# A gated cross-attention block on one core: the last two row pairs of the feed-forward part put into a written order

## The chip, the core and the metric

The kernel runs on one core of a Trainium2 chip. A core has five engines with a queue each: TensorE (PE in the profile; PEld is its weight load), VectorE (DVE), ScalarE (ACT), GpSimd (POOL), and SyncE (SP), which here only starts transfers. They run side by side and meet at semaphores. Inside one queue instructions run in the order of the program, so an instruction that waits holds up all that stand behind it on its engine. The metric is the device time of the whole kernel in microseconds; lower is better.

## What is computed

Sixteen sequences of 224 rows (512 wide) attend to a context of up to 750 rows (384 wide), of which a mask keeps only some; then each row passes a two-layer feed-forward net with quantised operands. Cut to what matters:

```python
def attention(x, context, mask, W_q, W_k, W_v, W_o, b_o):   # 8 heads of 64
    q, k, v = x @ W_q, context @ W_k, context @ W_v
    sim = where(mask, einsum(q, k) * 64**-0.5, -max)
    return einsum(softmax(sim), v) @ W_o + b_o

def bitlinear(x, w, b):
    xq = act_quant(rmsnorm(x))      # to 8-bit steps by the row's largest magnitude
    return xq @ weight_quant(w).T + b                       # weights to -1, 0, 1

def ffn(x): return bitlinear(gelu(bitlinear(x, w1, b1)), w2, b2)    # 512 -> 2048 -> 512

x = x + tanh(g_xattn) * attention(layernorm(x), context, ...)
x = x + tanh(g_ffn) * ffn(layernorm(x))
```

## The kernel before

**Work units.** The 16 sequences are ordered by how many context rows the mask keeps, and one sequence is a *slot* s (0 to 15). The 3584 rows in slot order are cut into 28 tiles of 128 rows; two tiles make a *pair* i (0 to 13), and k (0 or 1) is the tile within it. A slot's attention needs its queries, keys and values, the scores of four units (`scores`, L1088 and L1098), the turn of the probabilities by TensorE (`turn_probs`, L1128) and the weighted sum (`weighted`, L1151), whose result goes to the ring buffer `xoT`.

**What a pair passes through.** `residual` gathers the rows of x by an indirect transfer that GpSimd issues (L807) and adds the bias (L1207). `project(i, k)` multiplies `xoT` by W_o in float32 (L1214) and adds to the rows y (L1217). `normalise` takes mean and largest magnitude (L1251 to L1255), makes the quantising scale (`quantiser`, L1225 and L1226), rounds to integers (L1260) and turns them into bfloat16 (L1261); a transfer on SP's queue transposes them (L1262); GpSimd computes the scale that is multiplied back (`unquantiser`, L1233 to L1235). `up(i, k, g)` is the first layer for half g of 2048 columns (L1284), with a DVE add that takes the result out of PSUM (L1292). `gelu(i, ks)` runs Gelu on ACT (L1315), takes the largest magnitude (L1318), quantises (L1321), casts (L1324), transposes by a transfer on SP (L1325), and measures the mean square on ACT (L1344). `down` is the second layer (L1424, sixteen matmuls), and `store` adds into y (L1436) and sends the tile with an indirect transfer that GpSimd issues (L1438). The indirect stores wait for one another: each one waits until the store before it has landed.

**Two forms of a transpose.** The transposes of `xq` and `hq` go through a transfer on SP for most pairs. For the last two pairs, 12 and 13, `hq` is transposed by TensorE instead (`turn_by_tensor`: L1304, sixteen small matmuls, and two ACT copies at L1305).

**The order.** The main loop over slots hands three streams of pieces (attention of this slot; preparation of the next; feed-forward pieces of earlier pairs) to `merge`, which interleaves them by a planned cost each. In slot 15 the feed-forward stream is the residual of pair 12, `up` and `gelu` of pair 11, `project` and `normalise` of pair 12, and `down` of pair 11. After the loop comes the end, with what is left: the residual, projection and normalisation of pair 13; `up` of pair 12; `up_last` of pair 13 (as `up`, with Gelu and the largest magnitude by halves: L1366, L1374, L1377, L1378); `down` of pair 12 and of pair 13 with TensorE transposes woven in; four stores. The layer that builds the program still orders each engine's instructions by itself; `tc.issue_after(x)` keeps what is written in its block behind x on x's engine. It is order only and adds no semaphore.

Names of instructions below: `hp_12_0_1` is the up product of pair 12, tile 0, half 1; `fp` a down product; `op` a projection; `hq`, `hqT` the quantised middle rows and their transpose; `xq`, `xqT` the same for the input of the first layer; `c_2` the scale that `store` multiplies back.

Of the kernel before, what the change touches and what calls it, by code (L numbers as in the profile page):

```python
# [733 lines left out]
def compact_path(ctx, tc, sh, x, context, out, late_loads, stages):  # L734
# [405 lines left out]
    def weighted(s):  # L1140

        st = live[s]
        rest = CAPS[s] > P
        av = wide([P, 2, NB], F32, f"av_{s}")
        by = av[:, :, : 2 * S].rearrange("p a (i q) -> p a i q", i=2)
        for a in range(2):
            for i in range(2):
                p = 2 * a + i
                for j in range(2):
                    rows = slice((a ^ j) * DH, ((a ^ j) + 1) * DH)  # L1150
                    nc.tensor.matmul(  # L1151
                        by[rows, a, i, :],
                        lhsT=st["v"][:, (2 * p + j) * DH : (2 * p + j + 1) * DH],
                        rhs=st["pT"][:, 2 * p + j, :],
                        start=(i == 0),
                        stop=(not rest and i == 1),
                    )
        if rest:

            for i in range(2):  # L1160
                for a in range(2):
                    p = 2 * a + i
                    for j in range(2):
                        keys = slice(j * DH, (j + 1) * DH)
                        rows = slice((a ^ j) * DH, ((a ^ j) + 1) * DH)
                        nc.tensor.matmul(
                            by[rows, a, i, :],
                            lhsT=st["v_rest"][keys, p, :],
                            rhs=st["pT"][keys, 8 + p, :],
                            start=False,  # L1170
                            stop=(i == 1),
                        )
        at = (s % 4) * S
        for a in range(2):
            evict(xoT[:, 2 * a : 2 * a + 2, at : at + S], by[:, a], 2 * S)
# [33 lines left out]
    def project(i, k):  # L1209
        y = pairs[i]["y"]  # L1210
        at = (2 * i + k) * P % RING
        po = gen([P, D], F32, f"op_{i}_{k}")
        for d in range(ND):
            nc.tensor.matmul(  # L1214
                po, lhsT=xoT[:, d, at : at + P], rhs=sh.wo[:, d, :], start=(d == 0), stop=(d == ND - 1)
            )
        nc.vector.scalar_tensor_tensor(y[:, k, :], po, sh.tgates[:, 0:1], y[:, k, :], ALU.mult, ALU.add)  # L1217
        load["v"] += 700


# [9 lines left out]
    def unquantiser(amax, r, part, isw, name):  # L1230

        c = small(f"c_{name}")
        nc.gpsimd.tensor_tensor(c[:, part], amax[:, part], r[:, part], ALU.mult)  # L1233
        nc.gpsimd.tensor_scalar(c[:, part], c[:, part], 1e-5, None, ALU.max)
        nc.gpsimd.tensor_scalar(c[:, part], c[:, part], isw, None, ALU.mult)  # L1235
        return c

    def normalise(i, ks=(0, 1)):
# [20 lines left out]
        for k in ks:  # L1259
            nc.vector.tensor_scalar(xq.bitcast(I16)[:, k, :], fx[:, k, :], scale[:, k : k + 1], None, ALU.mult)  # L1260
        nc.vector.tensor_copy(xq[:, part, :], xq.bitcast(I16)[:, part, :])  # L1261
        nc.sync.dma_start_transpose(  # L1262
            out=xqT[:, ks[0] * ND : (ks[-1] + 1) * ND, :], in_=xq[:, part, :].rearrange("p n d -> p (n d)")
        )

# [7 lines left out]
        load["v"] += len(ks) * (850 + 340 + 667 + 450 + 220)  # L1273

    def up(i, k, g):
# [5 lines left out]
        for n in range(2):  # L1281
            at = (2 * g + n) * NB
            for d in range(ND):
                nc.tensor.matmul(  # L1284
                    ph[:, n, :],
                    lhsT=f["xqT"][:, k * ND + d, :],
                    rhs=w1T[:, d, at : at + NB],
                    start=(d == 0),
                    stop=(d == ND - 1),
                )  # L1290
# [3 lines left out]
        )  # L1294
        load["v"] += 1280

    def turn_by_tensor(i, k):
# [10 lines left out]
    def gelu(i, ks=(0, 1)):  # L1308
# [5 lines left out]
        for k in ks:  # L1314
            nc.scalar.activation(f["h", k], f["h", k], AF.Gelu)  # L1315
        for k in ks:
# [6 lines left out]
            if i < NPAIR - 2:  # L1323
                nc.vector.tensor_copy(hq, hq.bitcast(I16))  # L1324
                nc.sync.dma_start_transpose(out=hqT, in_=hq)  # L1325
                continue
            half = FF // 2
            for g in range(2):
                cols = slice(g * half, (g + 1) * half)
                nc.scalar.copy(hq[:, cols], hq.bitcast(I16)[:, cols])  # L1330
            f["hq", k] = hq
        f["ss", ks], f["a2", ks] = ss, amax
        if i < NPAIR - 2:
            measure(i, ks)
        load["v"] += len(ks) * (2282 + 1280 + 690)
        load["s"] += len(ks) * 2 * 1910 + 2600

    def measure(i, ks):
        f = pairs[i]
        name = f"{i}_{ks[0]}"  # L1340
        part = slice(ks[0], ks[-1] + 1)
        ss, amax = f["ss", ks], f["a2", ks]
        for k in ks:
# [5 lines left out]
        for k in ks:  # L1349
            f["c2", k] = c[:, k : k + 1]  # L1350

    def up_last(i, k):
# [8 lines left out]
        for g in range(2):  # L1361
            ph = wide([P, 2, NB], F32, f"hp_{i}_{k}_{g}")
            for n in range(2):
                at = (2 * g + n) * NB
                for d in range(ND):
                    nc.tensor.matmul(  # L1366
                        ph[:, n, :],
                        lhsT=f["xqT"][:, k * ND + d, :],
                        rhs=w1T[:, d, at : at + NB],
                        start=(d == 0),  # L1370
                        stop=(d == ND - 1),
                    )
# [5 lines left out]
            nc.vector.tensor_reduce(most[:, g : g + 1], h[:, cols], AX.X, ALU.max, apply_absolute_value=True)  # L1378
        f["h", k], f["most", k] = h, most

    def gelu_last(i, k):
# [11 lines left out]
        for g in range(2):  # L1393
            cols = slice(g * half, (g + 1) * half)
            nc.vector.tensor_scalar(hq.bitcast(I16)[:, cols], h[:, cols], scale[:, part], None, ALU.mult)
            rounded = nc.vector.tensor_copy(hq[:, cols], hq.bitcast(I16)[:, cols])
        f["hq", k], f["a2", k] = hq, amax
        return rounded.ins

    def measure_last(i, k):  # L1400
        f = pairs[i]
        name = f"{i}_{k}"
        part = slice(k, k + 1)
        squares = small(f"sq_{name}")
        for g in range(2):
# [6 lines left out]
            )  # L1412
        r = small(f"r2_{name}")
        nc.gpsimd.tensor_tensor(r[:, part], squares[:, 0:1], squares[:, 1:2], ALU.add)
        nc.gpsimd.tensor_scalar(r[:, part], r[:, part], 1.0 / FF, EPS, ALU.mult, ALU.add)
        pow_half(r[:, part])
        c = unquantiser(f["a2", k], r, part, sh.isw[1], f"2_{name}")
        f["c2", k] = c[:, part]

    def down(i, k, between=None):  # L1420
        f = pairs[i]
        po = gen([P, D], F32, f"fp_{i}_{k}")
        for n in range(NF):
# [3 lines left out]
            if between and n == NF // 2 - 1:  # L1427
                with tc.issue_after(last.ins):
                    f["turned"] = turn_by_tensor(*between)
        f["po", k] = po  # L1430

    def store(i, k):
        f = pairs[i]
        po = f["po", k]
        y = f["y"][:, k, :]
        nc.vector.scalar_tensor_tensor(y, po, f["c2", k], y, ALU.mult, ALU.add)  # L1436
        load["v"] += 700
        nc.gpsimd.indirect_dma_start(  # L1438
            out=out_rows,
# [4 lines left out]
            oob_is_err=False,  # L1444
        )
    NPAIR = NTOK // 2

# [14 lines left out]
    def project_pieces(i):  # L1462
        p = [(1.8, lambda k=k: project(i, k)) for k in range(2)]
        return p + [(0.0, lambda: normalise(i))]


# [177 lines left out]
    for s in range(B):  # L1644
# [10 lines left out]
        else:  # L1655
# [4 lines left out]
            if complete:  # L1660
                flow.append((0.0, lambda i=projected: residual(i)))
            if raised < projected:
                flow += up_pieces(raised)
                raised += 1
            if complete:
                flow += project_pieces(projected)
# [14 lines left out]
    residual(i)  # L1681
    for k in range(2):
        project(i, k)
        normalise(i, (k,))
    ups = up_pieces(i - 1)
    for k in range(2):
        for _, piece in ups[3 * k : 3 * k + 3]:
            piece()
    for k in range(2):
        up_last(i, k)  # L1690
    measure(i - 1, (0,))
    turn_by_tensor(i - 1, 0)
# [12 lines left out]
    store(i, 0)  # L1705
    with tc.issue_after(pairs[i]["turned"]):
        measure_last(i, 1)
    down(i, 1)
# [35 lines left out]
```

## Time and profile before

| | us |
|---|---|
| three timed runs: median (lowest to highest) | 751.87 (750.98 to 754.66) |
| the profiled execution, whole | 748.97 |
| its span, first to last instruction | 747.2 |
| start of the last store's issue, and its end | 734.90, 736.0 |
| from there to the end of the span (no compute instruction) | 11.2 |

| busy, us (share of the span) | PE | PEld | DVE | ACT | POOL |
|---|---|---|---|---|---|
| whole span | 682.8 (91%) | 436.8 (58%) | 497.6 (67%) | 420.0 (56%) | 396.4 (53%) |

Where a timeline row is shown, it gives the start in us from the start of the span, the duration in us, engine, line, operation, what it writes and reads (names without numbers), shapes, the count, and in brackets how long the engine had been idle before it and what ended the idle time. Times near the end of the span are what this change is about: it touches slot 15 (from about 648 us) and all that comes after it.

### The profile page before, as it was taken

What the parts mean: (1) busy time and instruction counts of PE and PEld (TensorE: products, weight loads), DVE (VectorE), ACT (ScalarE), POOL (GpSimd) and SP (SyncE); (2) the same over time, 40 slices, a digit from 0 to 9 for tenths busy, and PEclk for the clock granted to TensorE, in tenths of its full rate; (3) what the DMA queues carried; (4) which work ended last, traced back from release to release, by engine and by line L of the source; (5) the groups of instructions that cost most, each with busy time, mean ns of one, the idle gap of its engine ahead of it and who ended that gap; (6) DMA issues with size and microseconds to landing.
All of it is one profiled execution on the core that took longest, in us unless ns stands there. A gap on an engine that the chain in (4) does not pass through costs nothing.

```text
span 747.2 us, 11515 instructions
## 1 busy us (share of the span) xinstructions
PE 682.8 (91%) x3964; PEld 436.8 (58%) x3964; DVE 497.6 (67%) x1290; ACT 420.0 (56%) x981; POOL 396.4 (53%) x543
## 2 busy tenths in 40 slices
PE   4998899999999999997999999999999999988780
PEld 3786677675656565655555675666666566443330
DVE  5586846866684684755768675588594939586950
ACT  2549645383673846636757368366565656461680
POOL 5583676463654644547366564565654453536142
PEclk9989999999999999999999999999999999999996
DMA  7794031222222312222142323124122222213000
GB/s 244 272 292 130 29 87 32 15 73 57 81 45 60 95 43 73 52 59 80 28 100 68 78 61 68 42 68 85 55 57 71 57 71 54 75 29 78 7 26 35
DMA packets 78898, 56.67 MB, mean 76 GB/s; under 512 B 67168, under 2 KB 67312, under 8 KB 78704
## 3 DMA queue, kind: packets, MB, share of 16 engines
q1 hardware_dynamic: 70704, 29.90, 17.5%
q0 software_dynamic: 8128, 25.96, 10.9%
q8 instruction: 33, 0.54, 0.3%
q14 instruction: 33, 0.27, 0.1%
HBM read 32.26 MB, written 7.34 MB: 53 GB/s over the span
## 4 chain that ended last, share of the span: by engine, by line
PE 52%; DVE 13%; issue 12%; POOL 10%; ACT 6%; DMA 4%; POOLq 0%; ACTq 0%; DVEq 0%
PE qp L1035 9%; PE op L1214 8%; PE fp L1424 7%; PE hp L1284 6%; PE kp L916 4%; PE sim L1074 4%; PE vp L931 4%; PE ptp L1128 2%; PE av L1151 2%; POOL p L1108 2%; DVE a L1318 2%; DMA out_dram<-y,token 2%; DVE h L1292 2%; DVE hq L1321 1%; DVE p L1088 1%
## 5 line engine op out<-in xcount | busy, mean ns | idle before, releaser
L1108 POOL TENSOR_TENSOR p<-p,rec 112x768 f32<-112x768 f32 (+1 forms) x64 | 84.3, 1318 | 71.7 <-DVE rec L1107 29.1
L1098 ACT ACTIVATE p<-p,nm 112x192 f32<-112x192 f32 (+1 forms) x256 | 106.5, 419 | 8.0 <-DVE nm L1088 7.8
L1424 PE MATMUL fp<-w2T,hqT 128*128 128x512 fp8e4 x448 | 103.4, 384 | 7.9 <-ACT hqT L1305 4.0
L1035 PE MATMUL qp<-xnT,wq_sb 128*128 128x224 f32 x512 | 105.0, 359 | 0.6 <-ACT xnT L780 0.6
L1214 PE MATMUL op<-wo_sb,xoT 128*128 128x512 f32 x224 | 103.7, 599 | 0.0
L1284 PE MATMUL hp<-w1T,xqT 128*128 128x512 fp8e4 x416 | 99.8, 384 | 3.4 <-DVE nm L1088 1.9
L1035 PEld LDWEIGHTS qp<-xnT,wq_sb 128*128 128x128 f32 x512 | 96.9, 193 | 6.4 <-issue 3.3
L1292 DVE SCALAR_TENSOR_TENSOR h<-hp,c,b_bc 128x1024 f32<-128x1024 f32 x52 | 66.5, 1280 | 38.3 <-PE hp L1284 38.0
L1088 DVE CUSTOM_DVE_ANT_0 p<-sim,mask 112x128 f32<-112x128 f32 (+1 forms) x224 | 57.9, 313 | 34.0 <-PE sim L1074 33.7
L1424 PEld LDWEIGHTS <-hqT 128*128 128x128 bf16 x448 | 42.8, 99 | 62.4 <-issue 7.5
L1318 DVE TENSOR_REDUCE a<-h 128x1 f32<-128x2048 f32 x26 | 59.3, 2282 | 22.4 <-ACT h L1315 22.3
L1436 DVE SCALAR_TENSOR_TENSOR y<-fp,c,y 128x512 f32<-128x512 f32 x28 | 20.9, 746 | 78.0 <-PE fp L1424 66.5
L1284 PEld LDWEIGHTS <-xqT 128*128 128x128 bf16 x416 | 40.3, 98 | 48.6 <-issue 10.2
L1438 POOL DMA_INDIRECT out_dram<-y,token x28 | 30.7, 1095 | 62.6 <-DVE y L1436 51.6
L1214 PEld LDWEIGHTS op<-wo_sb,xoT 128*128 128x128 f32 x224 | 40.6, 190 | 38.9 <-issue 36.4
L916 PE MATMUL kp<-ctxT,wk_sb 128*128 128x192 f32 (+1 forms) x384 | 63.1, 313 | 0.0
L916 PEld LDWEIGHTS kp<-ctxT,wk_sb 128*128 128x128 f32 x384 | 57.5, 198 | 6.2 <-issue 4.3
L1344 ACT ACTIVATE h<-h 128x2048 f32<-128x2048 f32 x26 | 49.7, 1910 | 17.1 <-DVE hq L1321 9.6
L1272 POOL TENSOR_TENSOR y<-y,b_bc 128x512 f32<-128x512 f32 x28 | 36.6, 1312 | 38.3 <-DVE fx L1253 38.0
L780 ACT COPY pT<-ptp 128x448 f32<-128x448 f32 x62 | 32.3, 536 | 42.4 <-PE ptp L1128 42.3
L1315 ACT ACTIVATE h<-h 128x2048 f32<-128x2048 f32 x26 | 49.6, 1909 | 9.0 <-DVE h L1292 8.8
L1074 PE MATMUL sim<-kT,qT 64*112 64x192 f32 (+1 forms) x512 | 50.9, 313 | 1.0 <-DVE nm L1088 0.6
(195 smaller groups left out, 1223.3 us busy)
## 6 DMA issues: line engine op xcount, KB each, us to landing
raw<-in_L_ffn_w_dram SPq DMA_DIRECT2D x16, 512.0 KB, 5.3
wq_sb<-in_L_xattn_W_q_dram SPq DMA_DIRECT2D x1, 1024.0 KB, 5.7
b_bc<-in_L_ffn_b_dram SPq DMA_DIRECT2D x1, 1024.0 KB, 8.0
wk_sb<-in_L_xattn_W_k_dram SPq DMA_DIRECT2D x1, 768.0 KB, 7.3
wv_sb<-in_L_xattn_W_v_dram SPq DMA_DIRECT2D x1, 768.0 KB, 8.7
wo_sb<-in_L_xattn_W_o_dram SPq DMA_DIRECT2D x1, 512.0 KB, 3.7
wo_sb<-in_L_xattn_W_o_dram SPq DMA_DIRECT2D x2, 256.0 KB, 5.7
y<-in_x_dram,token POOLq DMA_INDIRECT x28, 3.5
```

Source lines behind the costliest of these rows:

```text
L916: nc.tensor.matmul(pk[:, p - p0, :], lhsT=sh.wk[:, c, p * P : (p + 1) * P], rhs=st["ctxT"][:, c, :cap], start=(c == 0), stop=(c == NC - 1),)
L1035: nc.tensor.matmul(pq[:, i, :], lhsT=sh.wq[:, d, (p + i) * P : (p + i + 1) * P], rhs=st["xnT"][:, d, :], start=(d == 0), stop=(d == ND - 1),)
L1074: nc.tensor.matmul(sim[:, j, i, :cap], lhsT=st["qT"][j * DH : (j + 1) * DH, p, q * TQ : (q + 1) * TQ], rhs=st["kT"][j * DH : (j + 1) * DH, ...
L1088: nc.vector.tensor_tensor_reduce(out=probs[:, h, :cap], in0=sim[:, j, i, :cap], in1=st["mask"][:, j * begin : j * begin + cap], scale=-(DH ...
L1098: nc.scalar.activation(probs[:, h, :cap], probs[:, h, :cap], AF.Exp, bias=nmax, scale=-1.0, accum_out=total[:TQ, h : h + 1],)
L1108: nc.gpsimd.tensor_tensor(probs[:, :, :cap], probs[:, :, :cap], rec[:TQ].unsqueeze(2).to_broadcast([TQ, 4, cap]), ALU.mult,)
L1214: nc.tensor.matmul(po, lhsT=xoT[:, d, at : at + P], rhs=sh.wo[:, d, :], start=(d == 0), stop=(d == ND - 1))
L1284: nc.tensor.matmul(ph[:, n, :], lhsT=f["xqT"][:, k * ND + d, :], rhs=w1T[:, d, at : at + NB], start=(d == 0), stop=(d == ND - 1),)
L1292: nc.vector.scalar_tensor_tensor(h[:, cols], ph.rearrange("t i n -> t (i n)"), f["c1", k], sh.b1[:, cols], ALU.mult, ALU.add)
L1318: nc.vector.tensor_reduce(amax[:, k : k + 1], h, AX.X, ALU.max, apply_absolute_value=True)
L1344: nc.scalar.activation(f["h", k], f["h", k], AF.Square, accum_out=ss[:, k : k + 1])
L1424: last = nc.tensor.matmul(po, lhsT=f["hqT", k][:, n, :], rhs=w2T[:, n, :], start=(n == 0), stop=(n == NF - 1))
```

## The change

The last slot's feed-forward stream and the end are written out as one sequence. Pair 12 goes up in front of the projection of pair 13; its down product is split around the way up of pair 13; pair 11's second down product moves out of slot 15 into the end; the input rows of pair 13 are transposed by TensorE (`turn_rows`) instead of by a transfer, and tile 0 of pair 12's middle rows by a transfer instead of by TensorE. The mean square of h_12_1 and of pair 13 is computed apart from the scale that is multiplied back (`mean_square`, `measure_last`). `project`, `up`, `up_last`, `down`, `normalise` and `store` return instructions, so that later ones can be put behind them. Lines that only do that are left out here, and so is `gelu_last`, where a return value goes.

```diff
@@ normalise
-        nc.sync.dma_start_transpose(
-            out=xqT[:, ks[0] * ND : (ks[-1] + 1) * ND, :], in_=xq[:, part, :].rearrange("p n d -> p (n d)")
-        )
+        if i < NPAIR - 1:
+            nc.sync.dma_start_transpose(
+                out=xqT[:, ks[0] * ND : (ks[-1] + 1) * ND, :], in_=xq[:, part, :].rearrange("p n d -> p (n d)")
+            )
...
+    def turn_rows(i, k):
+
+        f = pairs[i]
+        pt = gen([P, ND, P], BF16, f"xqp_{i}_{k}")
+        for d in range(ND):
+            nc.tensor.transpose(pt[:, d, :], f["xq"][:, k, d * P : (d + 1) * P], ident16)
+        nc.scalar.copy(f["xqT"][:, k * ND : (k + 1) * ND, :], pt)
@@ gelu
         for k in ks:
-            nc.scalar.activation(f["h", k], f["h", k], AF.Gelu)
+            if (i, k) != (NPAIR - 2, 1):
+                nc.scalar.activation(f["h", k], f["h", k], AF.Gelu)
...
             if i < NPAIR - 2:
-                nc.vector.tensor_copy(hq, hq.bitcast(I16))
+                late["rounded"] = nc.vector.tensor_copy(hq, hq.bitcast(I16)).ins
+            else:
+                for g in range(2):
+                    cols = slice(g * FF // 2, (g + 1) * FF // 2)
+                    nc.scalar.copy(hq[:, cols], hq.bitcast(I16)[:, cols])
+            f["hq", k] = hq
+            if (i, k) != (NPAIR - 2, 1):
                 nc.sync.dma_start_transpose(out=hqT, in_=hq)
...
+        if (i, ks[0]) == (NPAIR - 2, 1):
+            f["a2", 1] = amax[:, 1:2]
+            return
@@ down
             if between and n == NF // 2 - 1:
                 with tc.issue_after(last.ins):
-                    f["turned"] = turn_by_tensor(*between)
+                    between()
@@ new
+    def last_slot(i):
+
+        ups = up_pieces(i - 1)
+
+        def norm(k):
+            late["normed"] = normalise(i, (k,))
+
+        def gelu_behind():
+            with tc.issue_after(late["normed"]):
+                gelu(i - 1, (1,))
+
+        p = ups[:5]
+        for k in range(2):
+            p += [(1.8, lambda k=k: project(i, k)), (0.0, lambda k=k: norm(k))]
+        return p + [(0.0, gelu_behind)] + down_pieces(i - 1)[:1]
@@ the slot loop
-            if raised < projected:
+            if s == B - 1:
+                flow += last_slot(projected)
+            elif raised < projected:
@@ the end
     i = NPAIR - 1
     residual(i)
-    for k in range(2):
-        project(i, k)
-        normalise(i, (k,))
-    ups = up_pieces(i - 1)
-    for k in range(2):
-        for _, piece in ups[3 * k : 3 * k + 3]:
-            piece()
-    for k in range(2):
-        up_last(i, k)
-    measure(i - 1, (0,))
-    turn_by_tensor(i - 1, 0)
-    down(i - 1, 0, (i - 1, 1))
-    down(i - 1, 1)
-    with tc.issue_after(pairs[i - 1]["turned"]):
-        measure(i - 1, (1,))
-    rounded = [gelu_last(i, k) for k in range(2)]
-    for k in range(2):
-        with tc.issue_after(rounded[k]):
-            store(i - 1, k)
-    with tc.issue_after(pairs[i - 1]["turned"]):
+    with tc.issue_after(late["av"]), tc.issue_after(late["rounded"]):
+        for k in range(2):
+            for g in range(2):
+                raised = up(i - 1, k, g)
+            if k == 0:
+                gelu(i - 1, (0,))
+    f = pairs[i - 1]
+    nc.scalar.activation(f["h", 1], f["h", 1], AF.Gelu)
+    mean_square(i - 1, 1)
+    with tc.issue_after(raised):
+        lowered = down(i - 2, 1)
+    store(i - 2, 1)
+    with tc.issue_after(lowered):
+        for k in range(2):
+            projected = project(i, k)
+            normed = normalise(i, (k,))
+    with tc.issue_after(normed):
+        gelu(i - 1, (1,))
+    measure_last(i - 1, 1)
+    with tc.issue_after(projected):
+        lowered = down(i - 1, 0, lambda: turn_rows(i, 0))
+    with tc.issue_after(lowered):
+        up_last(i, 0)
+        mean_square(i, 0)
+        turn_rows(i, 1)
+        raised = up_last(i, 1)
+    store(i - 1, 0)
+    with tc.issue_after(raised):
+        turn_by_tensor(i - 1, 1)
+        lowered = down(i - 1, 1)
+    mean_square(i, 1)
+    added, sent = store(i - 1, 1)
+    gelu_last(i, 0)
+    with tc.issue_after(added):
+        gelu_last(i, 1)
+    with tc.issue_after(raised):
+        turn_by_tensor(i, 0)
+    with tc.issue_after(sent):
         measure_last(i, 0)
-    turn_by_tensor(i, 0)
-    down(i, 0, (i, 1))
-    store(i, 0)
-    with tc.issue_after(pairs[i]["turned"]):
-        measure_last(i, 1)
+        measured = measure_last(i, 1)
+    with tc.issue_after(lowered):
+        down(i, 0, lambda: turn_by_tensor(i, 1))
+    with tc.issue_after(measured):
+        store(i, 0)
     down(i, 1)
     store(i, 1)
```

`mean_square` holds the two ACT squares of half a tile and the three GpSimd steps up to the inverse root, which stood at the head of `measure_last` before.

More of the change, by code (lines that the diff above doesn't have):

```diff
@@ L1150, in weighted @@
                     rows = slice((a ^ j) * DH, ((a ^ j) + 1) * DH)
-                    nc.tensor.matmul(
+                    last = nc.tensor.matmul(
                         by[rows, a, i, :],
@@ L1165, in weighted @@
                         rows = slice((a ^ j) * DH, ((a ^ j) + 1) * DH)
-                        nc.tensor.matmul(
+                        last = nc.tensor.matmul(
                             by[rows, a, i, :],
@@ L1172, in weighted @@
                         )
+        late["av"] = last.ins
         at = (s % 4) * S
@@ L1213, in project @@
         for d in range(ND):
-            nc.tensor.matmul(
+            last = nc.tensor.matmul(
                 po, lhsT=xoT[:, d, at : at + P], rhs=sh.wo[:, d, :], start=(d == 0), stop=(d == ND - 1)
@@ L1218, in project @@
         load["v"] += 700
+        return last.ins
     def quantiser(amax, part, least, name):
@@ L1234, in unquantiser @@
         nc.gpsimd.tensor_scalar(c[:, part], c[:, part], 1e-5, None, ALU.max)
-        nc.gpsimd.tensor_scalar(c[:, part], c[:, part], isw, None, ALU.mult)
+        latest["p"] = nc.gpsimd.tensor_scalar(c[:, part], c[:, part], isw, None, ALU.mult).ins
         return c
@@ L1260, in normalise @@
             nc.vector.tensor_scalar(xq.bitcast(I16)[:, k, :], fx[:, k, :], scale[:, k : k + 1], None, ALU.mult)
-        nc.vector.tensor_copy(xq[:, part, :], xq.bitcast(I16)[:, part, :])
-        nc.sync.dma_start_transpose(
-            out=xqT[:, ks[0] * ND : (ks[-1] + 1) * ND, :], in_=xq[:, part, :].rearrange("p n d -> p (n d)")
-        )
+        rounded = nc.vector.tensor_copy(xq[:, part, :], xq.bitcast(I16)[:, part, :])
+        if i < NPAIR - 1:
+            nc.sync.dma_start_transpose(
+                out=xqT[:, ks[0] * ND : (ks[-1] + 1) * ND, :], in_=xq[:, part, :].rearrange("p n d -> p (n d)")
+            )
         r = small(f"r1_{name}")
@@ L1273, in normalise @@
         load["v"] += len(ks) * (850 + 340 + 667 + 450 + 220)
+        return rounded.ins
+    def turn_rows(i, k):
[4 more added lines that the diff above has]
+        nc.scalar.copy(f["xqT"][:, k * ND : (k + 1) * ND, :], pt)
     def up(i, k, g):
@@ L1283, in up @@
             for d in range(ND):
-                nc.tensor.matmul(
+                last = nc.tensor.matmul(
                     ph[:, n, :],
@@ L1295, in up @@
         load["v"] += 1280
+        return last.ins
     def turn_by_tensor(i, k):
@@ L1323, in gelu @@
             if i < NPAIR - 2:
-                nc.vector.tensor_copy(hq, hq.bitcast(I16))
-                nc.sync.dma_start_transpose(out=hqT, in_=hq)
[L1326 to L1342, printed above, removed]
+                late["rounded"] = nc.vector.tensor_copy(hq, hq.bitcast(I16)).ins
[5 more added lines that the diff above has]
+            if (i, k) != (NPAIR - 2, 1):
+                nc.sync.dma_start_transpose(out=hqT, in_=hq)
+        if (i, ks[0]) == (NPAIR - 2, 1):
+            f["a2", 1] = amax[:, 1:2]
+            return
         for k in ks:
@@ L1350, in measure @@
             f["c2", k] = c[:, k : k + 1]
+        load["v"] += len(ks) * (2282 + 1280 + 690)
+        load["s"] += len(ks) * 2 * 1910 + 2600
     def up_last(i, k):
@@ L1365, in up_last @@
                 for d in range(ND):
-                    nc.tensor.matmul(
+                    last = nc.tensor.matmul(
                         ph[:, n, :],
@@ L1379, in up_last @@
         f["h", k], f["most", k] = h, most
+        return last.ins
     def gelu_last(i, k):
@@ L1395, in gelu_last, with mean_square @@
             nc.vector.tensor_scalar(hq.bitcast(I16)[:, cols], h[:, cols], scale[:, part], None, ALU.mult)
[L1396 to L1400, printed above, removed]
+            nc.vector.tensor_copy(hq[:, cols], hq.bitcast(I16)[:, cols])
+        f["hq", k], f["a2", k] = hq, amax[:, part]
+    def mean_square(i, k):
         f = pairs[i]
         name = f"{i}_{k}"
-        part = slice(k, k + 1)
         squares = small(f"sq_{name}")
@@ L1412, in measure_last @@
             )
[L1413 to L1418, printed above, removed]
+        f["r2", k] = r = small(f"r2_{name}")
+        nc.gpsimd.tensor_tensor(r[:, 0:1], squares[:, 0:1], squares[:, 1:2], ALU.add)
+        nc.gpsimd.tensor_scalar(r[:, 0:1], r[:, 0:1], 1.0 / FF, EPS, ALU.mult, ALU.add)
+        pow_half(r[:, 0:1])
+    def measure_last(i, k):
+        f = pairs[i]
+        c = unquantiser(f["a2", k], f["r2", k], slice(0, 1), sh.isw[1], f"2_{i}_{k}")
+        f["c2", k] = c[:, 0:1]
+        return latest["p"]
     def down(i, k, between=None):
@@ L1428, in down @@
                 with tc.issue_after(last.ins):
-                    f["turned"] = turn_by_tensor(*between)
+                    between()
         f["po", k] = po
+        return last.ins
     def store(i, k):
@@ L1435, in store @@
         y = f["y"][:, k, :]
-        nc.vector.scalar_tensor_tensor(y, po, f["c2", k], y, ALU.mult, ALU.add)
+        added = nc.vector.scalar_tensor_tensor(y, po, f["c2", k], y, ALU.mult, ALU.add)
         load["v"] += 700
-        nc.gpsimd.indirect_dma_start(
+        sent = nc.gpsimd.indirect_dma_start(
             out=out_rows,
@@ L1445, in store @@
         )
+        return added.ins, sent.ins
     NPAIR = NTOK // 2
@@ L1661, in compact_path @@
                 flow.append((0.0, lambda i=projected: residual(i)))
-            if raised < projected:
+            if s == B - 1:
+                flow += last_slot(projected)
+            elif raised < projected:
                 flow += up_pieces(raised)
                 raised += 1
-            if complete:
+            if complete and s < B - 1:
                 flow += project_pieces(projected)
```

## The prediction

> **What bounds the kernel now.** The change begins in slot 15, so I read the stretches from there first: start and end in us, length, busy time (and count) of PE, PEld, DVE, ACT and POOL, granted TensorE clock, DMA share, GB/s.
>
> ```profile
> 652.00:680.30 28.30, 22.54 (x113) 10.93 (x111) 21.71 (x46) 15.08 (x30) 14.01 (x20) 1.00 0.29 54
> 680.30:712.00 31.70, 27.16 (x129) 12.29 (x127) 27.67 (x38) 14.74 (x14) 7.61 (x17) 1.00 0.08 24
> 712.00:722.90 10.90, 7.26 (x37) 3.39 (x38) 7.62 (x18) 9.69 (x13) 6.59 (x16) 0.84 0.00 0
> 722.90:736.00 13.10, 6.92 (x44) 3.42 (x42) 1.50 (x2) 4.01 (x6) 5.84 (x10) 0.88 0.18 65
> ```
>
> PE and DVE share the load up to 712; afterwards no engine is full. Then the timeline of the end:
>
> ```profile
> 722.92 1.12 POOL L1438 DMA_INDIRECT out_dram<-y,token  x1 [0.48 <-issue]
> 726.55 0.97 POOL L1438 DMA_INDIRECT out_dram<-y,token  x1 [2.52 <-DMA out_dram<-y,token]
> 730.71 0.97 POOL L1438 DMA_INDIRECT out_dram<-y,token  x1 [3.19 <-DMA out_dram<-y,token]
> 733.87 0.75 DVE L1436 SCALAR_TENSOR_TENSOR y<-fp,c,y 128x512 f32<-128x512 f32 x1 [6.64 <-POOL c L1235]
> 734.90 1.10 POOL L1438 DMA_INDIRECT out_dram<-y,token  x1 [1.07 <-DVE y L1436]
> ```
>
> Four stores, each begun after the one before has landed, 3.6 to 4.2 us apart. The last add waits 6.64 us, for a scale that stands behind the third store in GpSimd's queue; the last matmul had ended at 729.8 (5.34 us of them from 724.48). So the stores' queue, not the matmuls, sets the end, by about 4 us. Last, from the timeline and the chain of waits, what the way there is made of:
>
> ```profile
> 669.98 1.93 POOL L1108 TENSOR_TENSOR p<-p,rec 112x512 f32<-112x512 f32 x1 [0.98 <-DVE rec L1107]
> 671.08 1.38 DVE L1324 CAST hq<-hq 128x2048 bf16<-128x2048 int16 x1
> 672.52 4.26 DMA hqT<-hq
> 676.83 3.63 PE L1424 MATMUL fp<-w2T,hqT 128*128 128x512 fp8e4 x16 [1.84 <-DMA hqT<-hq]
> 680.29 7.03 PE L1214 MATMUL op<-wo_sb,xoT 128*128 128x512 f32 x16
> 714.93 5.31 PE L1424 MATMUL fp<-w2T,hqT 128*128 128x512 fp8e4 x16 [2.98 <-ACT hqT L1305]
> ```
>
> The DVE cast ends at 672.46, its transposing transfer takes 4.26 us, fp of pair 11 follows, then the projection of pair 13 at 680.29. Sixteen down matmuls take 3.63 us there, 5.31 us at 714.93, after an idle of 2.98 us. The third is a clock effect, the pair of rows at 670 a stall; both return below.
>
> **The change, costed.** The built order of each engine shows that the new sequence is really there, so I follow it on the clock of the old trace. Up to 652 nothing moves.
>
> *Slot 15 until the projection of pair 13: later by 5.3 us.* PE's queue now holds, in front of that projection, all four up products of pair 12 and the second down product of pair 11. The last of these waits for a transfer, hqT_11_1, that SP issues behind the two half-size transposes of xq_12 (about 1.2 us of issue each, done by then), once DVE has made hq_11_1. DVE now works without a gap from the scores of units 2 and 3: its first of eight mask steps starts at about 656.7 (PE's scores of unit 2). Steps, with durations from the groups and timeline, less the 0.08 us by which the next independent one overlaps: eight mask steps at 0.21, 1.7; largest magnitude of h_11_0 2.2, scale 0.3, quantise 1.2, cast 0.6; two reciprocals and the second up add of h_11_1 (1.28) 1.4; pair 12's rows in two halves, each y add 0.75, statistics 0.68 and 0.15, subtract 0.49, maximum 0.69, scale 0.31, quantise 0.49, cast 0.29, together 6.8; the store add of fp_11_0 0.7; for h_11_1 again 2.2, 0.3, 1.2, 0.7. Sum 19.3, so 676.0 before stalls.
>
> Stalls: at 671.08 the cast took 1.38 us instead of the usual 0.69, because the GpSimd multiply ran until 671.91; that multiply had itself started at 669.98 and waited for the DVE quantise before it. Four quantising or casting DVE steps of the new sequence meet a GpSimd multiply or add of 1.05 to 1.27 us. The Trainium skill, "GPSIMD Engine Reference", Specifications, says that the two engines share their SBUF interfaces and contend when DVE runs a two-port mode or reads two SBUF inputs. The rule would charge the first-layer quantises and the store adds alike; in this trace DVE adds with one operand in PSUM kept 0.75 us beside GpSimd. By the rule, nine steps at up to 0.7, 6 us; by the row, four at 0 to 0.7, so 0 to 2.8. I take 1.8, nearer to the row. Cast done at 677.8, transfer 4.3, landing 682.1; the up products of pair 12 end there too, since each half waits for DVE to empty one of two buffers. Then fp_11_1, 3.5 to the next matmul: projection at 685.6 against 680.29.
>
> *Projection to the add of fp_12_1: 29.6 us.* The casts of hq_12_0 go to ACT and its transpose to SP: quantise 1.3, two casts 2.0, transfer 4.3, latencies 0.4 give +8.0, one microsecond after the projections' 7.0; PE idles between. Then 16 down matmuls 3.5, four transposes and an ACT copy (half of the 1.01 us copy of L1305) 1.1: +12.6. These replace the transposing transfers of xq_13 at about 2.7 us each. The first tile of pair 13 goes up in 3.5: +16.1. The largest magnitude of h_12_1 (2.28), put behind normalise, keeps DVE busy to about the same time; two adds to +18.7, one half-tile maximum 1.2 and the quantise of h_12_1 1.2 to +21.1. ACT has two Gelus (1.06) and two squares (1.16) in front of the casts: casts start +21.9, and casts, copies and the two Gelus of the second tile, 0.95 each, end at +27.6; half of fp_12_1 1.8 and the add's latency: +29.6, or 715.2.
>
> *From there to the end: 15.0 us, and 1.7 for the clock.* The add stands in front of pair 13's quantise on DVE: 0.7, scales 0.5, quantise of two halves 1.4, first cast 0.45, eight transposes and latency 0.75, ACT copy 1.0, eight down matmuls 1.8: 6.6. In it, pair 13's second tile is quantised. Sixteen transposes 0.9, eight matmuls 1.7, sixteen 3.5 with latency: 12.9. Add 0.75, issue 1.4: 15.0. GpSimd's scales (put behind the store of 12_1 by order, about 0.3 us each, some six of them) are done 5 us before they are needed, so they cost nothing; without that cover, they would cost at most the 2.1 us that one such chain took at 731.7. The store of 13_0 starts at +10.4; landing and reissue at the old spacing of 3.6 to 4.2 let the last start at +14.0 to +14.6, against +13.9 by its data: 0.1 to 0.7 more, I take 0.2.
>
> PE idles for about 3.2 us while that quantise runs. The Trainium skill, "TensorE: Matmul & The Clock Gate", Part 1, speaks against such a gap: free-running windows of about 3.4 us, half rate after an idle one until a busy one has passed. The row at 714.93 shows 1.7 us lost after 2.98 us. By the rule a gap of 3.2 us need not hold a whole window, so 0, or two windows with the small transposes counted as idle, 3.4; by the row 1.7, which I take since the row's gap is nearly as long. On the old path this loss was hidden by the stores; on the new one matmuls set the end, so it counts.
>
> Sum: 685.6 + 29.6 + 15.0 + 0.2 + 1.7 = 732.1 against 736.0, a gain of 3.9. A check: the last matmul would end at 729.8, as before; the gain is the stores' queue. Of the profiled execution, 748.97, with 1.8 us around the span and 11.2 behind the last issue unchanged, this leaves 745.1; the median of the runs shown stands 2.9 above that execution, and I put the gain on it: 751.87 - 3.9, **748.0 us**. What a measurement can tell from no change is about 0.5%, 3.8 us: 748.1 is the border.
>
> **The rivals.** *The clock is low twice* (also before fp_12_1, after an idle near 2 us while hq_12_1 is cast): 1.7 more, 749.7. For it: the late part is thin on PE; against it: the gap of 1.84 us at 674.99 cost nothing. *Clear way*: no stall (1.8) and full clock (1.7), 744.5; for it, two of the later cast rows had no stall; against it, the multiplies are there. *Slower*: the DVE and GpSimd collision in slot 15, since DVE's chain now stands ahead of the last projection. The worst cast of the kernel took 3.26 us, 2.57 over the usual; four such are 10.3 instead of 1.8, 756.5. Against it: in that stretch the worst was 0.69. It decides from 5.7 us of stalls. That the change does nothing is excluded by the order: the store of 11_1 and the first two of the last four leave the end.
>
> **How the numbers follow.** The sum as told 0.56, own range 746.6 to 749.2; low clock twice 0.27; clear way 0.09; slower 0.08. The range 745.0 to 750.8 leaves out the slower case, half of the clear way and a little of the low clock. Faster by over 0.5%: of the first case, evenly about the border and leaning to it where the stores' spacing is short, 0.42, with the clear way 0.51; within 0.5%: 0.14 and 0.27, 0.41; slower 0.08.
>
> **What would show it.** Right: projection of pair 13 at 684 to 687; the add of fp_12_1 at 714 to 717; the last add released by PE and not by GpSimd; only two stores behind 722; eight or more late fp matmuls 0.43 us apart. Wrong: casts in slot 15 of 2 us and more, a projection after 689, or last stores that still wait for each other by over 1 us.

## The result and the profile after

The changed kernel takes 748.71 us (median of ten runs, 745.8 to 750.15) against 751.76 us for the kernel before, timed beside it (ten runs, 749.35 to 754.66). The ratio is 0.9956, with a 95% interval of 0.9937 to 0.9974: 3.3 us less, between 2.0 and 4.7 (the two medians alone differ by 3.05). The prediction was 748.0, 3.9 us less.

The two profiled executions differ by less. That of the changed kernel took 748.71 us, its median (span 746.8); that of the kernel before took 748.97 (span 747.2), less than all of its timed runs. So the traces cannot be compared by their ends alone; first the tail itself. The windows of the changed kernel, with the columns of the prediction's first fence, are cut where the granted clock changes:

```profile
652.00:686.50 34.50, 30.29 (x148) 14.59 (x147) 30.47 (x59) 19.88 (x33) 16.68 (x29) 1.00 0.24 54
686.50:710.07 23.57, 19.00 (x82) 8.38 (x80) 19.51 (x32) 14.89 (x20) 12.04 (x28) 1.00 0.18 45
710.07:716.90 6.83, 6.01 (x20) 2.54 (x21) 3.21 (x3) 5.73 (x8) 0.85 (x3) 0.50 0.01 2
716.90:720.30 3.40, 1.08 (x5) 0.29 (x3) 2.18 (x8) 0.00 (x0) 1.23 (x3) 1.00 0.00 0
720.30:727.10 6.80, 5.72 (x29) 3.26 (x30) 3.28 (x8) 1.93 (x2) 2.95 (x6) 0.50 0.10 39
727.10:735.40 8.30, 6.02 (x38) 2.91 (x36) 1.50 (x2) 1.93 (x2) 2.03 (x2) 1.00 0.11 39
```

TensorE runs at half clock (0.50) twice in the end, for 6.8 us each; the kernel before had one such stretch of 3.4 us while TensorE had work (the 0.84 of the prediction's third window; the 0.88 of its fourth is a stretch behind the last matmul). What that does to the work is seen in TensorE's timeline:

```profile
686.51 7.03 PE L1215 MATMUL op<-wo_sb,xoT 128*128 128x512 f32 x16
...
711.91 6.07 PE L1435 MATMUL fp<-w2T,hqT 128*128 128x512 fp8e4 x16 [0.82 <-ACT hqT L1318]
721.13 1.89 PE L1317 MATMUL hqp<-ident,hq 128*128 128x128 bf16 x16 [3.15 <-DVE hq L1405]
723.26 3.60 PE L1435 MATMUL fp<-w2T,hqT 128*128 128x512 fp8e4 x8 [0.25 <-ACT hqT L1318]
726.65 1.29 PE L1317 MATMUL hqp<-ident,hq 128*128 128x128 bf16 x16
727.78 5.34 PE L1435 MATMUL fp<-w2T,hqT 128*128 128x512 fp8e4 x24
```

Sixteen matmuls of fp_12_1 take 6.07 us instead of 3.6, eight of fp_13_0 3.60 instead of 1.9. In front of the second stretch TensorE stood idle for 3.15 us, waiting for DVE's cast of hq_13_0. The stores, in the timeline of the end:

```profile
718.09 0.75 DVE L1448 SCALAR_TENSOR_TENSOR y<-fp,c,y 128x512 f32<-128x512 f32 x1 [4.02 <-PE fp L1435]
...
719.13 1.11 POOL L1450 DMA_INDIRECT out_dram<-y,token  x1 [2.14 <-DVE k L1227]
...
730.82 1.06 POOL L1450 DMA_INDIRECT out_dram<-y,token  x1 [7.48 <-DVE y L1448]
733.23 0.75 DVE L1448 SCALAR_TENSOR_TENSOR y<-fp,c,y 128x512 f32<-128x512 f32 x1 [2.70 <-PE fp L1435]
734.40 0.97 POOL L1450 DMA_INDIRECT out_dram<-y,token  x1 [2.52 <-DVE y L1448]
```

Two stores stand behind 722, and the last add is released by TensorE (2.70 us waited for fp). The row of the last store names that add as well, but the chain that ended last goes through the landing of the store before:

```profile
730.82 2.81 DMA out_dram<-y,token
...
733.67 0.51 issue
734.18 0.04 POOLq L250
...
734.40 0.97 POOL out_dram L1450
```

The landing came at 733.63 and the store began 0.77 us later, as the stores at 726.55 and 730.71 of the kernel before did after theirs (725.78 and 729.94). A store that an add alone released began 0.28 us after it (730.82 here, 734.90 before), and this add ended at 733.98. So the last store waited about 0.1 us for a landing. Otherwise the bound has passed from the stores' queue to TensorE, and TensorE lost time to the clock.

### The profile page after: what moved, and what is told of

It is laid out like the page before. It is cut to its first block, busy times and chain, and to the rows that moved or that the text cites. A ratio compares the mean times of both kernels' runs of the same rounds, so it can differ in the third digit from the quotient of the medians.

```text
span 746.8 us, 11509 instructions
## 1 busy us (share of the span) xinstructions
PE 686.4 (92%) x3956; PEld 438.6 (59%) x3956; DVE 497.9 (67%) x1294; ACT 419.8 (56%) x983; POOL 396.6 (53%) x549
## 4 chain that ended last, share of the span: by engine, by line
PE 55%; issue 12%; POOL 11%; DVE 11%; ACT 5%; DMA 3%; POOLq 0%; ACTq 0%; DVEq 0%
PE qp L1035 9%; PE op L1215 9%; PE fp L1435 8%; PE hp L1296 6%; PE sim L1074 4%; PE kp L916 4%; PE vp L931 4%; PE av L1151 3%; POOL p L1108 2%; PE ptp L1128 2%; DVE a L1332 2%; POOL x L807 2%; ACT p L1098 1%; DVE ind L830 1%; DVE p L1088 1%
## 5 line engine op out<-in xcount | busy, mean ns | idle before, releaser
L1435 PE MATMUL fp<-w2T,hqT 128*128 128x512 fp8e4 x448 | 105.5, 390 | 2.9 <-DMA hqT<-hq 1.8
L1350 ACT ACTIVATE h<-h 128x2048 f32<-128x2048 f32 x25 | 47.7, 1910 | 18.0 <-DVE hq L1335 12.5
L1329 ACT ACTIVATE h<-h 128x2048 f32<-128x2048 f32 x25 | 47.7, 1909 | 6.3 <-DVE h L1304 6.1
```

Of the source, the lines that this page charges most:

```text
L1435: last = nc.tensor.matmul(po, lhsT=f["hqT", k][:, n, :], rhs=w2T[:, n, :], start=(n == 0), stop=(n == NF - 1))
```

## A measure that the start of the kernel does not blur

Executions differ before the change begins: the last projection tile in front of slot 15, the same work in all kernels here, started between 626.93 and 631.54, at 627.92 in the profile before and at 628.91 in the one after. So I count from the start of that tile to the start of the projection of pair 13 (*way to 13*), and from there to the start of the last store's issue (*end*). All are starts in the timelines, one execution each. Each ratio is against runs of the kernel before on the same chip (medians 751.5 to 751.8).

| kernel | median, us | ratio to before (95%) | way to 13 | end | sum |
|---|---|---|---|---|---|
| before | 751.76 | 1 | 52.37 | 54.61 | 106.98 |
| changed | 748.71 | 0.9956 (0.9937 to 0.9974) | 57.60 | 47.89 | 105.49 |
| changed, again | 748.16 | 0.9951 (0.9929 to 0.9973) | 57.62 | 44.54 | 102.16 |
| before, one store less | 747.57 | 0.9940 (0.9921 to 0.9959) | 52.47 | 51.43 | 103.90 |
| changed, one store less | 747.77 | 0.9950 (0.9929 to 0.9970) | 59.25 | 46.59 | 105.84 |
| before, stores first | 748.50 | 0.9970 (0.9949 to 0.9991) | 53.75 | 51.58 | 105.33 |
| before, TensorE kept busy | 751.79 | 1.0008 (0.9986 to 1.0031) | 53.79 | 54.54 | 108.33 |
| changed, TensorE kept busy | 746.25 | 0.9926 (0.9902 to 0.9951) | 57.54 | 43.49 | 101.03 |
| quantise ahead | 743.19 | 0.9892 (0.9865 to 0.9920) | 57.45 | 40.84 | 98.29 |
| quantise ahead, again | 742.79 | 0.9889 (0.9868 to 0.9910) | 59.21 | 41.50 | 100.71 |
| second order | 744.53 | 0.9905 (0.9878 to 0.9932) | 59.23 | 42.44 | 101.67 |
| third order | 741.22 | 0.9869 (0.9841 to 0.9898) | 59.19 | 39.36 | 98.55 |

A half-rate stretch also falls into slot 15 in some executions, of either kernel: the rows with 53.75 and 53.79 (against 52.4) and with 59.2 (against 57.5) have one there. It costs 1.4 to 1.8 us and does not come from the edits: the quantise ahead has one in one execution and none in the other.

## The experiments

### Did the stores set the end before, and not after?

The store of tile 1 of pair 12 is left out in both kernels (its rows are not written; the rest is computed). In the changed kernel the return hands back the add in the store's place.

```diff
+        if (i, k) == (NPAIR - 2, 1):
+            return
         nc.gpsimd.indirect_dma_start(
```

> The kernel before, with the store of the second tile of pair 12 left out (the rows of that tile are not written; all else is computed). My theory: the row of four stores, 3.6 to 4.2 us apart, sets the end of the kernel before. With three, the store of 13_0 can issue at 727.4, the last scale's chain of 2.1 us follows at 728.5 and is done at 730.6, the last matmul ends at 729.8, so the last store issues near 731.6 instead of 734.9: 3.3 us less, ratio 0.9956 (748.5 us if before is 751.8). Rival (matmuls set the end, the stores only fill the time): 0 to 0.5 us less, ratio 0.9995.

> The changed kernel, with the same store left out (the rows of the second tile of pair 12 are not written). My theory: here the store of 12_1 issues at 719.1 and the next one at 730.8, 11.7 us later, so nothing waits for it: the same time as the changed kernel within 0.5 us, ratio to the kernel before 0.9956 and not lower than 0.994. Rival (the stores' queue still sets the end after the change): another 2 to 4 us less, ratio 0.990 to 0.993.

Measured: before, 0.9940 (0.9956 expected, inside the interval) and an end of 51.43 instead of 54.61, 3.2 us less (expected 3.3). After, 0.9950, the changed kernel's own ratio within the noise, with an end of 46.59 that lies between its two others. So the row of stores set the end before, and after it the store of tile 12_1 no longer counts. This settles the prediction's first step, the bound; the 0.1 us between the last two stores is out of this experiment's reach.

### Is the stores' queue enough to explain the gain?

The kernel before, its old sequence untouched; only GpSimd's queue is reordered, so that each store of pair 12 stands behind its own scale. The lines that split `measure` and `measure_last`, so that their GpSimd part can be put behind a store, are left out.

```diff
-    with tc.issue_after(pairs[i - 1]["turned"]):
-        measure(i - 1, (1,))
     rounded = [gelu_last(i, k) for k in range(2)]
-    for k in range(2):
-        with tc.issue_after(rounded[k]):
-            store(i - 1, k)
+    with tc.issue_after(rounded[0]):
+        sent = store(i - 1, 0)
+    with tc.issue_after(pairs[i - 1]["turned"]):
+        measure(i - 1, (1,), sent)          # its GpSimd part behind `sent`
+    with tc.issue_after(rounded[1]):
+        sent = store(i - 1, 1)
     with tc.issue_after(pairs[i - 1]["turned"]):
-        measure_last(i, 0)
+        measure_last(i, 0, sent)
```

> The kernel before with its old sequence and nothing of the change but a shorter end of GpSimd's queue: the store of 12_0 stands directly behind its scale, the store of 12_1 directly behind its own, and the scales of pair 13 follow. My theory (the serial stores set the end of the kernel before): the first store issues near 718 instead of 722.9, the second near 723.5, the third at 727.4, then the last scale's chain of 2.1 us to 730.6, and the last store at 731.7 instead of 734.9: 3.2 us less, ratio 0.9957, and from the projection of pair 13 to the last store 51.4 us instead of 54.6. Rival (the gain of the change came from the new place of the last projection, not from the stores): no more than 0.5 us less, ratio 0.9995, 54 us or more from the projection to the last store.

Its stores and adds in the timeline:

```profile
718.57 1.34 POOL L1459 DMA_INDIRECT out_dram<-y,token  x1 [1.07 <-DVE y L1457]
...
722.98 1.10 POOL L1459 DMA_INDIRECT out_dram<-y,token  x1 [1.07 <-DVE y L1457]
...
727.91 1.12 POOL L1459 DMA_INDIRECT out_dram<-y,token  x1 [1.68 <-DVE y L1457]
731.22 0.75 DVE L1457 SCALAR_TENSOR_TENSOR y<-fp,c,y 128x512 f32<-128x512 f32 x1 [3.60 <-POOL c L1235]
732.26 1.10 POOL L1459 DMA_INDIRECT out_dram<-y,token  x1 [1.08 <-DVE y L1457]
```

Counted from the projection of pair 13, the first store goes at 37.9 us instead of 42.6, each store starts when its sum is there, and the end is 51.58 us, 3.0 less (expected 51.4). The timed runs say 2.3 us less by the ratio, between 0.7 and 3.8; the ratio expected, 0.9957, is inside. Moving pair 12's stores forward is thus enough for a gain that the timing does not tell apart from that of the whole written sequence; on the old sequence a few lines do it. That the last add still waits for its scale (3.60 us on GpSimd) is what is left of that queue.

### Does the clock cost the changed kernel, and not the kernel before?

Matmuls whose product nobody reads fill TensorE's idles: in the changed kernel 7 and 13, in the kernel before 12.

```diff
+    def warm(n, name):
+        pt = gen([P, D], F32, name)
+        for j in range(n):
+            last = nc.tensor.matmul(pt, lhsT=ident16, rhs=w2T[:, j, :], start=True, stop=True)
+        return last.ins
@@ changed kernel
+    with tc.issue_after(raised):
+        raised = warm(7, "warm_a")
     with tc.issue_after(raised):
         turn_by_tensor(i - 1, 1)
@@
-    with tc.issue_after(raised):
+    with tc.issue_after(lowered):
+        warmed = warm(13, "warm_b")
+    with tc.issue_after(warmed):
         turn_by_tensor(i, 0)
@@ kernel before
     down(i - 1, 0, (i - 1, 1))
+    warm(12, "warm")
     down(i - 1, 1)
```

> The kernel before with 12 unused matmuls in TensorE's idle of 2.98 us in front of fp_12_1. My theory: full clock there, sixteen matmuls in 3.7 instead of 5.3 us, but the stores hide it: from the projection of pair 13 to the last store 54.6 us as before within 0.5, ratio 1.000 (0.998 to 1.002). Rival (the clock sets the end of the kernel before too): 1.7 us less, 52.9 us from the projection to the last store, ratio 0.9977.

> The changed kernel with TensorE kept busy by matmuls whose product is not used: 7 (1.5 us) before the transposes of hq_12_1, 13 (2.8 us) before those of hq_13_0, each inside an idle of 1.61 and 3.15 us. My theory: the two stretches of half rate, each 6.8 us long in the changed kernel, cost it 6.07 - 3.5 + 0.4 = 3.0 us and 0.9 + 1.8 + 0.3 = 3.0 us, and they are brought on by the idles; then the granted clock stays at full to the last matmul and the last store issues 5 to 6 us earlier: ratio to before 0.987 to 0.989 (742.5 to 743.5 us). Rival (the clock falls for another reason, or the low clock is hidden by DVE and the stores): the same as the changed kernel or up to 0.5 us more, ratio 0.9956 to 0.996.

> The changed kernel unchanged, for a second look at where the half-rate stretches fall. My theory: their place against the work differs between executions, since they start on a free-running raster; with both stretches full, as in its first profile, the projection of pair 13 to the last store takes 47.9 us, with none some 43.5; another execution lies between, 44 to 48, and the ratio to before is 0.9956 within 0.002. Rival (the stretches are tied to the work): again 47.9 within 0.2 us, sixteen matmuls of fp_12_1 in 6.07 us.

Before: fp_12_1 took 3.63 instead of 5.31 us, and the end stayed 54.54 against 54.61. The clock loss was hidden by the stores, as the prediction had it. After: with TensorE kept busy the clock stays at full, and the end is 43.49. The same kernel without the extra matmuls had 47.89 in its first profile and 44.54 in its second, where TensorE's timeline shows why:

```profile
714.56 3.75 PE L1435 MATMUL fp<-w2T,hqT 128*128 128x512 fp8e4 x16 [1.24 <-ACT hqT L1318]
721.67 1.51 PE L1317 MATMUL hqp<-ident,hq 128*128 128x128 bf16 x16 [3.36 <-DVE hq L1405]
723.43 2.92 PE L1435 MATMUL fp<-w2T,hqT 128*128 128x512 fp8e4 x8 [0.25 <-ACT hqT L1318]
```

fp_12_1 ran at full clock there, and the second stretch was 3.4 us long instead of 6.8. So the loss is 47.89 - 43.49 = 4.4 us in one execution, 1.05 in another, 3.1 in a third (the one with a store less, 46.59). My expectation of 5 to 6 us for the timed gain was too high twice over: it added the row lengths (6.0), of which 4.4 reached the end, and it took the unluckiest execution for the usual one. The medians differ by 2.5 us, near the mean of the three losses, 2.9.

### What takes the idle of 3.15 us off TensorE?

DVE waited 4.02 us for fp_12_1 with the quantise of pair 13 standing behind that add (row 718.09 above), and TensorE then waited for the quantise. The order is turned round:

```diff
-    added, sent = store(i - 1, 1)
     gelu_last(i, 0)
-    with tc.issue_after(added):
-        gelu_last(i, 1)
+    rounded = gelu_last(i, 1)
+    with tc.issue_after(rounded):
+        added, sent = store(i - 1, 1)
```

> The changed kernel with one order turned round: DVE quantises both tiles of pair 13 in front of the add of fp_12_1, not behind it. DVE idles 4.02 us there while it waits for fp_12_1. My theory: then the transposes of hq_13_0 can follow fp_12_1 at once, the idle of 3.15 us on TensorE goes, and with it the second stretch at half rate (3.0 us), as the first is left: 5 to 6 us less than the changed kernel, ratio 0.987 to 0.989. If the clock falls all the same: 2.5 to 3 us less, ratio 0.9915. Rival (the later add and store of 12_1 hold up the scales on GpSimd and the last stores): no gain, ratio 0.9956 or above.

> The quantise ahead alone, a second time, for a look at the clock in another execution and a comparison on the same chip. My theory: its idles on TensorE are 1.6 and 0.7 us, too short to hold a stretch of the raster without work, so the clock stays at full from the projection of pair 13 on: 40.8 us to the last store within 0.5, ratio 0.989 within 0.0025. Rival (its first profile was luck with the raster): a half-rate stretch there, 42.5 us or more.

TensorE's timeline of the first of the two:

```profile
711.35 3.75 PE L1436 MATMUL fp<-w2T,hqT 128*128 128x512 fp8e4 x16 [1.23 <-ACT hqT L1318]
715.80 1.07 PE L1317 MATMUL hqp<-ident,hq 128*128 128x128 bf16 x16 [0.69 <-DVE hq L1405]
717.52 1.90 PE L1436 MATMUL fp<-w2T,hqT 128*128 128x512 fp8e4 x8 [0.66 <-ACT hqT L1318]
```

The idle is 0.69 us, both stretches are gone in this execution, and the ratios 0.9892 and 0.9889 stand at the edge of what was expected (0.987 to 0.989): by the ratios 4.8 us less than the changed kernel, and faster than either of the two kernels compared here. Against the kernel kept busy, whose clock was full too, the end is 2.6 us shorter (40.84 and 43.49): that is the order itself, and the rest of the gain is the clock. The second execution shows that I was wrong to call the clock safe: fp_12_1 took 5.31 us in it, the end 41.50 instead of 40.84. The rival had named 42.5 or more, so neither figure was met.

### Can more be had behind it, and where does it stop?

Of the edits, only lines that set the order are shown, first those that both kernels have. The second order also moves ACT's casts and copies of pair 12 in front of squares and Gelus, and each quantise to its magnitude; the third differs only in the add of fp_12_1, which stands in front of the quantise of 13_1 instead of behind it.

```diff
+    rounded = gelu_last(i, 0)
+    with tc.issue_after(turned), tc.issue_after(rounded):
+        for half in later:                  # Gelu and magnitude of h_13_1, by halves
+            most = gelu_half(*half)
+        mean_square(i, 0)
@@ second order
+    rounded = gelu_last(i, 1)
+    with tc.issue_after(rounded):
+        added, sent = store(i - 1, 1)
@@ third order
+    with tc.issue_after(most):
+        added, sent = store(i - 1, 1)
+    with tc.issue_after(added):
+        gelu_last(i, 1)
```

> The changed kernel with its end reordered further: DVE quantises tile 13_0 as soon as its largest magnitude is there and tile 13_1 after its own, both in front of the add of fp_12_1, and ACT casts hq_12_1 and copies hqT_12_1 in front of the squares and of the Gelus of 13_1. My theory: the quantise takes the idle off TensorE (as with the quantise ahead alone, ratio 0.989), and the casts start 0.8 us earlier and the copies end 1 to 1.5 us earlier: 1.5 to 2.5 us less than with the quantise ahead alone, from the projection of pair 13 to the last store 38.5 to 39.5 us against 40.8, ratio 0.986 to 0.987. Rival (DVE, by now without a gap, or the three stores at the old spacing of 3.6 to 4.2 us become the bound): 40.5 us or more, ratio 0.989.

> As the further reordered end, with one order put right: in that kernel the stores had become the bound (issued at 720.98, 725.24 and 730.62, the last add done at 726.9), since the add of fp_12_1 stood behind both quantises. Here it stands between the last magnitude of tile 13_1 and its quantise, some 2.5 us earlier. My theory: the store of 12_1 issues near 718, that of 13_0 when its sum is there, and only the last waits for one landing: from the projection of pair 13 to the last store 39 to 40 us instead of 42.4, ratio 0.986 to 0.988. Rival (the three stores stay 4.3 to 5.4 us apart and bind, or the quantise of 13_1, 0.75 us later, holds up TensorE by as much as is gained): 41 us or more, ratio 0.989 or above.

The second order gained nothing over the quantise ahead (end 42.44, expected 38.5 to 39.5), and the timeline of its stores shows the rival, the stores' spacing:

```profile
720.98 1.11 POOL L1457 DMA_INDIRECT out_dram<-y,token  x1 [2.94 <-DVE y L1455]
...
725.24 1.12 POOL L1457 DMA_INDIRECT out_dram<-y,token  x1 [0.48 <-DVE y L1455]
726.11 0.75 DVE L1455 SCALAR_TENSOR_TENSOR y<-fp,c,y 128x512 f32<-128x512 f32 x1 [1.41 <-PE fp L1442]
730.62 0.98 POOL L1457 DMA_INDIRECT out_dram<-y,token  x1 [4.26 <-DMA out_dram<-y,token]
```

Its last sum is there at 726.86, but the last store waits 4.26 us for the landing of the one before, which took 4.61 us from its start instead of the 2.7 to 3.4 of other late stores. With the add of fp_12_1 earlier, the third order:

```profile
717.60 1.11 POOL L1457 DMA_INDIRECT out_dram<-y,token  x1 [0.25 <-DVE k L1227]
...
723.23 1.12 POOL L1457 DMA_INDIRECT out_dram<-y,token  x1 [0.49 <-DVE y L1455]
725.53 0.75 DVE L1455 SCALAR_TENSOR_TENSOR y<-fp,c,y 128x512 f32<-128x512 f32 x1 [2.70 <-PE fp L1442]
726.87 0.98 POOL L1457 DMA_INDIRECT out_dram<-y,token  x1 [2.52 <-DVE y L1455]
```

Counted from the projection of pair 13, the first store is 2.7 us earlier (30.1 instead of 32.8), the landing in front of the last store took 2.87 us again, and the end is 39.36 (expected 39 to 40). The last store still began 0.77 us after a landing (726.10) and 0.59 after its add, so by some 0.3 us it waits for the store before it. Of the 3.1 us between these two ends 1.7 are the slow landing, and the order's share is not separated further. At 741.22 us, ratio 0.9869, the third has the lowest median of all, by the ratios 6.5 us below the changed kernel; its interval overlaps that of the quantise ahead, so between those two the timing does not decide.

## Why the prediction was right, by its own steps

**The marks.** The projection of pair 13 at 686.51 (684 to 687 named), the last add released by TensorE, two stores behind 722, and well over eight late matmuls at half rate came as named; the add of fp_12_1 did not. (On the old trace's clock, 0.99 us lower in this execution, the projection is at 685.5.)

**The bound.** Right, and shown: with one store less the end of the kernel before is 3.2 us shorter, and the changed kernel gains nothing.

**Slot 15, +5.3 us.** Measured 57.60 - 52.37 = 5.2, and 57.62, 57.54, 57.45 in three other executions of that front. Inside, two terms were off and in part cancelled, which was luck: the DVE chain from the first mask step (657.69) to the end of the cast of hq_11_1 (678.36) was 20.7 us against 19.3 + 1.8 = 21.1. Of the 1.8 for DVE and GpSimd colliding, one stall is seen:

```profile
671.32 1.27 POOL L1275 TENSOR_TENSOR y<-y,b_bc 128x512 f32<-128x512 f32 x1
671.44 1.44 DVE L1262 TENSOR_SCALAR xq<-fx,k 128x512 int16<-128x512 f32 x1
```

The quantise takes 1.44 us instead of 0.48 while a GpSimd add runs: 0.96. The other 0.4 was small steps and gaps outside the list, not told apart. Being 0.4 us early brought nothing: the transfer landed at 682.68, but fp_11_1 began at 683.06, when the last up product of pair 12 let TensorE go. Of the two readings weighed there, nine steps at 0.7 is out, and the row's 0 to 2.8 holds. The DVE chain at 661 to 665 shows another outcome: the cast at 662.95 kept its 0.69 us, and the GpSimd multiply beside it took 1.54 instead of 1.04.

**Projection to the add of fp_12_1, 29.6 us.** At full clock it is 29.26 (changed kernel, again) and 29.27 (kept busy). In the first profile 31.58, the 2.3 us over being the half rate in fp_12_1. So the prediction's mark "714 to 717" for that add was missed (718.09) by the clock alone.

**From there to the end of the last issue, 15.0 + 0.2.** With TensorE kept busy 733.06 - 717.87 = 15.19. The stores' share, 0.2, was there at about 0.1: in that execution too the last store began 0.77 us after a landing and 0.41 after its add, where an add alone takes 0.28.

**The clock, 1.7 us.** This is the step that failed in size. It was taken from one row, as one loss in one place; measured 4.4, 1.05 and 3.1 us in three executions, in up to two places. A single piece of 3.41 us at half rate cost 1.05 to 1.55 us, and two joined ones 2.3 and 2.1. So 1.7 was near the price of one stretch; what went wrong was to count one. The rival "the clock is low twice" is what happened in two of the three executions.

Together: without any loss the sum promised 3.9 + 1.7 = 5.6 us, and the kernel kept busy has 106.98 - 101.03 = 5.95 in its profile and 5.6 in the timed runs (0.9926). Less the mean loss of 2.9 in place of 1.7, 5.95 leaves 3.05, near the 3.3 of the ratio. So the forecast of 3.9 was 0.6 to 0.8 too good through the clock, within its range of 745.0 to 750.8; the size of the mean rests on three executions, and where the stretches fell in any one of them was chance. The rival that ended slower needed 5.7 us of stalls and found 0.96.

## What to carry to other kernels

Serial stores at the end are a queue of their own: count them, multiply by their pitch, and look whether the last one waits for a landing or for its sum before anything is done to the matmuls. When a bound is taken away, the losses that it had covered (here the half-rate stretches behind thin TensorE work) begin to count, so price them for the new path and as a spread over executions, not from one row. An engine that idles in front of an instruction with ready work queued behind it (DVE's 4.02 us) is an order to turn round; that one turn brought 4.8 us on top of the rewritten sequence's 3.3.

## What the runs showed of the hardware

**When the clock falls and returns.** The half-rate stretches came in pieces of 3.41 us on a raster that the work does not move: in the changed kernel's trace the changes of the clock at 351.67 and 710.07 lie 105 such pieces apart. I cut the last 100 us of all twelve traces on that raster, up to the last matmul. Of the pieces at full rate, each one in which TensorE was busy for less than 1.45 us was followed by half rate, and none with more than 1.66. Between the two, busy time did not decide: in the changed kernel a piece with 1.48 us (from 706.65) was followed by half rate and one with 1.45 (from 675.93) was not; in the quantise ahead one with 1.66 was followed by it in one execution and one with 1.64 not in the other. Earlier in the kernel, near 202 us, pieces with 2.2 us of work were followed by half rate too, so busy time alone is no rule. The Trainium skill, "TensorE: Matmul & The Clock Gate", Part 1, speaks of an idle window; in these traces a window need not be idle. In the same last stretch a half-rate piece with 2.34 or 2.59 us of work was followed by another, one with 2.70 or more by full rate. Hence the two lengths, and hence the same idle of 1.6 us in front of fp_12_1 costing 2.3 us in one execution and nothing in the next.

**The pitch of the stores.** Where one store waited for the other they stood 3.5 to 4.2 us apart: 2.7 to 3.4 from the start of the first to its landing, and 0.77 from there to the start of the next. The last two of the second order stood 5.4 apart, all of the difference in the landing; what made it slow is open.
